# A four-layer image kernel on one core: the diagonal of a scan moved to ACT, pieces of a pipeline at other places, two softplus operations on POOL

## The chip, the cores and the metric

The program runs on one core of a Trainium2 chip. The core has five engines that run side by side, each through its own instructions in order: PE (TensorE: matrix products and, as PEld, the loading of their weights), DVE (VectorE), ACT (ScalarE), POOL (GpSimd) and SP (SyncE, which here issues DMA transfers and does no arithmetic). They wait for each other by semaphores. SBUF is the working memory of 128 partitions, PSUM the memory that PE writes into; POOL works on SBUF alone.

The metric is the device time of one execution in microseconds (us), smaller being better. Of the kernel before there are ten timed runs: the median is 7649.24 us, the lowest 7633.43 and the highest 7655.76.

## The reference, cut to what matters

Four layers follow each other on an input of 4 images with 96 channels and 64 x 64 pixels, all in 32-bit floating point. The change touches layers 0 and 1; layer 2 (two windowed attentions and an MLP) and layer 3 (Fourier magnitudes, a deformable convolution) stay as they are.

Layer 0 runs two state-space blocks over the 4096 pixels of an image taken as a sequence:

```python
h = (seq - mu) * rsqrt(var + EPS) * ln_g + ln_b
xs, z = split(h @ in_w)                       # 192 channels each
xc = silu(causal 4-tap convolution of xs + conv_b)
dt, Bm, Cm = split(xc @ xproj_w)              # 6, 16 and 16 columns
delta = softplus(dt @ dt_w + dt_b)
dA  = exp(delta * A)                          # 192 channels x 16 states
dBx = delta * Bm * xc
hstates[t] = dA[t] * hstates[t-1] + dBx[t]    # a scan along the sequence
y = sum over states of hstates * Cm + Dp * xc
seq = seq + (y * silu(z)) @ out_w
```

After both blocks come a product with fus_w, a batch norm and the residual. Dp is a vector over the channels: "Dp * xc" is a product with a diagonal matrix.

Layer 1 is a depthwise 5 x 5 convolution with silu, and then a smaller state-space form with 4 states:

```python
delta = softplus(dt_w @ dts + dt_b)
log_dA = maximum(delta * A, log(1e-9))
P = exp(cumsum(log_dA))
hs = P * cumsum(delta * Bs * xs / maximum(P, 1e-9))
y = sum over states of hs * Cs + xs * Ds
```

Both softplus functions are computed as relu(v) + log(1 + exp(-|v|)), with a correction: w = 1 + e is rounded, and e - (w - 1), what the rounding lost, is given back. So there is a relu (dl or dx), a term w - 1 - e that is subtracted from it, and a logarithm that is added to it.

## The kernel before, in words

**Layer 0** works in units. A unit is one image, one of the two blocks and one chunk of 512 pixels: 4 x 2 x 8 = 64 units, one after the other. Its 192 x 16 states lie in 24 tiles of 128 partitions x 512: eight steps m = 0 to 7, in each of which three tiles (index q) lie side by side. Even steps serve channels 0 to 95 (hf = 0), odd ones channels 96 to 191, and two steps share one of four groups of states (nq).

One step is, in the order of the data: DVE multiplies the replicated input xR by the broadcast Bb into a tile bt of 128 x 1536 (L577); ACT computes three decays a_ps = exp(A * dR) (L588); DVE runs three scans over bt (L604), each with one decay; ACT copies the last column to the carry (L612); POOL multiplies bt by Cb (L613); PE sums the states into yp (L630, "collect"). bt has four buffers and a_ps three.

The order of the work is written out by hand: the program's order is the order of each engine's queue. Every step has four quarters q = 0 to 3. Quarters 0 to 2 issue a scan each, and then the decay of the scan two places on. Quarter 3 issues the sums of two steps earlier (`collect(v - 2)`), then the carry and L613 of this step (`outputs`), and then L577 of the next (`inputs`).

What a unit needs before its scans is made by the generator `prepare`, whose pieces end at each `yield`. Piece n of a unit's preparation runs at the head of quarter n - 16, counted in quarters from the start of the unit before it: one piece in each quarter, over two units, an empty piece being a pause. The condition is `taken[w] <= 4 * v + q - PERIOD * (w - 1) + AHEAD`, with a PERIOD of 32 quarters and 16 AHEAD. In order, the pieces that the prediction names, with the places (step, quarter) that they have before:

- (4,0) PE product L418; (4,2) ACT L423 and L424; (4,3) PE L427 and a small copy on POOL, L432; (5,1) ACT L435 and L436; (5,2) DVE L438; (5,3) ACT L440; (6,0) to (6,3) the convolution's products, PE L447; from (7,0) ACT L456 and PE L459, by turns.
- In the next unit: (0,0) to (0,2) ACT L463, L466, then L468 with L469; (0,3) ACT L471 and POOL L472, the silu's last product; (1,2) PE L478; (2,0) ACT L482 and a store by SP; (2,1) PE L488; (2,3) two ACT L495 (the absolute values of softplus); (3,0) ACT L497 (exponential) and L498 (relu of the first half); (3,1) L500 (relu of the second half) and two L502 (the 1 + e); (3,2) two DVE L505 (w - 1 - e); (3,3) two ACT L511 (logarithms) and POOL L512; (4,0) POOL L514 and stores by SP; (4,1) POOL L519 and stores by SP; (4,2) ACT L524; (4,3) ACT L526 and the six loads dR and xR of the first half by SP; (5,0) ACT L531 and POOL L532.

Beside these, at fixed places: L641 (yp of the unit before, to SBUF by ACT) at (1,1) and (2,1), POOL L646 at (2,2) and then the products L650 and L652 and what follows them, and the loads of the second half and of Cb from (5,2) on. In three units `pooled` puts a long reduction (L400) on DVE. At the first chunk of every image and block `collect` makes the diagonal `skips[hf]` = ident * Dp with a DVE operation (L624), which PE multiplies by xc (L627).

**Layer 1** works in 16 chunks of 1024 pixels, with three tiles each: 48 steps v, i = v mod 3. In a step `sums` does the first cumulative sum of the next step (DVE L902, a product and a maximum, and the scan L903, whose other input is a broadcast one; POOL L907; ACT L908 to L910; POOL L911), and `states` the second one of this step (DVE L925, the scan L926, ACT L929, DVE L930 and L933, and PE's sums L937 and spreads L319). L950 ends a chunk. Around them lie three places n = 0, 1, 2: place 0 is before `sums`, place 1 between `sums` and `states`, place 2 after `states`.

The preparation of a chunk has nine pieces: 1 transposes (PE L857); 2 silu (ACT L862) with the loading of its table and of the next one; 3 a product (PE L319); 4 absolute value, exponential and 1 + e (ACT L874 to L876); 5 relu (DVE L878); 6 w - 1 - e (DVE L880) and its subtraction (L881); 7 the logarithm (ACT L883); 8 its addition (DVE L885) and six loads of rl by SP; 9 the product dx (POOL L889) and six loads of rx by SP. The set `slots` gives the places, with the step counted from the first step of the chunk before.

Of the kernel before, what the change touches and what calls it, by code (L numbers as in the profile page):

```python
# [12 lines left out]
AF = mybir.ActivationFunctionType  # L13
ALU = mybir.AluOpType
# [4 lines left out]
B, C, H, W = 4, 96, 64, 64  # L19
# [320 lines left out]
def layer0(k, X):  # L340

    tc, nc, ins = k.tc, k.nc, k.ins
# [4 lines left out]
    with ExitStack() as es:  # L347
# [46 lines left out]
        def mm():  # L394
            return pm.tile([128, NB], F32, name="mm_ps", tag="mm")
# [18 lines left out]
        def prepare(b, i, ch, st, before):  # L414
# [6 lines left out]
            e = p2.tile([C, 2, T], F32, name="e")  # L421
# [13 lines left out]
            nc.scalar.activation(p[:C], p[:C], AF.Ln, bias=k.eps5[:C])  # L435
            nc.scalar.activation(p[:C], p[:C], AF.Exp, scale=-0.5)  # L436
            yield
            nc.vector.scalar_tensor_tensor(d, d, k.v(f"ln_g{i}"), p[:C], ALU.mult, ALU.mult)  # L438
            yield
            nc.scalar.activation(h[:, 3:], d, AF.Identity, bias=k.v(f"ln_b{i}"))  # L440
# [2 lines left out]
            ps = []  # L443
# [42 lines left out]
            ps = [mm() for _ in range(2)]  # L486
# [4 lines left out]
            e = p2.tile([C, 2, T], F32, name="e")  # L491
            dx = p1.tile([C, 2, T], F32, name="dx")
            bias = [k.v(f"dt_b{i}{hf}") for hf in range(2)]
            for hf, p in enumerate(ps):
                nc.scalar.activation(e[:, hf], p[:C], AF.Abs, bias=bias[hf])  # L495
            yield
            nc.scalar.activation(e, e, AF.Exp, scale=-1.0)  # L497
            nc.scalar.activation(dx[:, 0], ps[0][:C], AF.Relu, bias=bias[0])  # L498
            yield
            nc.scalar.activation(dx[:, 1], ps[1][:C], AF.Relu, bias=bias[1])  # L500
            for hf, p in enumerate(ps):
                nc.scalar.activation(p[:C], e[:, hf], AF.Identity, bias=k.one[:C])  # L502
            yield
# [5 lines left out]
            w = p1.tile([C, 2, T], F32, name="w")  # L509
# [46 lines left out]
        carries, bts, Bbs, dec, skips = {}, {}, {}, {}, {}  # L556

        def at(v):

            u, m = divmod(v, NT)  # L560
            return (sts[u], units[u], *divmod(m, 2))
# [55 lines left out]
        def collect(v):  # L617

            st, (b, i, ch), nq, hf = at(v)
            if nq == 0:  # L620
                yp = st["yp", hf] = py.tile([C, T], F32, name="yp")
                if ch == 0:
                    skips[hf] = p1.tile([C, C], F32, name=f"skip{hf}")
                    nc.vector.tensor_scalar(  # L624
                        skips[hf], k.ident[:C, :C], k.v(f"Dp{i}{hf}"), None, ALU.mult
                    )
                nc.tensor.matmul(yp, skips[hf], st["xc"][:, hf], start=True, stop=False)  # L627
            bt = bts.pop(v)
            for q in range(NG):
                nc.tensor.matmul(  # L630
                    st["yp", hf][32 * q : 32 * q + 32],
                    red,
                    bt[:, q],
                    start=False,
                    stop=nq == NQ - 1,
                )
# [92 lines left out]
        scale, shift = batch_norm(k, wp, stats, k.v("bn_g"), k.v("bn_b"))  # L729
# [11 lines left out]
def batch_norm(k, pool, stats, gamma, beta):  # L741

    nc = k.nc
    mv = pool.tile([C, 2], F32, name="bn_mv")
    nc.vector.bn_aggr(mv, stats.rearrange("c b n s -> c (b n s)"))
    sc = pool.tile([C, 2], F32, name="bn_sc")
    nc.scalar.activation(sc[:, 0:1], mv[:, 1:2], AF.Sqrt, bias=k.eps5[:C])
    nc.vector.reciprocal(sc[:, 0:1], sc[:, 0:1])
    nc.vector.tensor_mul(sc[:, 0:1], sc[:, 0:1], gamma)
    nc.vector.tensor_mul(sc[:, 1:2], mv[:, 0:1], sc[:, 0:1])  # L750
    nc.vector.tensor_sub(sc[:, 1:2], beta, sc[:, 1:2])
    return sc[:, 0:1], sc[:, 1:2]
# [5 lines left out]
def layer1(k, X):  # L758

    tc, nc, ins = k.tc, k.nc, k.ins  # L760
    T, G, NT = 1024, 8, 3
    NP, NCH = H // 2, L // T
    with ExitStack() as es:
# [10 lines left out]
        with tc.tile_pool(name="l1s", bufs=1) as sp, tc.tile_pool(  # L774
# [4 lines left out]
            ps = pp.tile([C, C], F32, name="wd1_ps")  # L779
# [4 lines left out]
        with tc.tile_pool(name="l1t", bufs=3) as tp, tc.tile_pool(  # L784
# [11 lines left out]
            for i in range(B * NP // 4):  # L796
                b, p0 = divmod(4 * i, NP)
                ps = pp.tile([128, 4, C], F32, name="ft_ps", tag="t")
# [8 lines left out]
            for g in range(C // G):  # L807
                t = bands.pop(0)
                for h in range(2):
                    c0 = G * g + 4 * h  # L810
                    ps = pp.tile([128, 4, B, NP], F32, name="cv_ps", tag="t")
# [29 lines left out]
        def packed(dst, src):  # L841

            for n in range(4):
                r = C * n
                while r < C * n + C:
                    at = r % 128
                    m = min(C * n + C - r, 128 - at)
                    c0 = r - C * n
                    nc.sync.dma_start(dst[r // 128][at : at + m], src[c0 : c0 + m])
                    r += m  # L850

        def prepare(u):

            b, ch = divmod(u, NCH)
            ps = pm.tile([C, T], F32, name="xs_ps", tag="mm")
            for j in range(T // 128):
                nc.tensor.transpose(  # L857
                    ps[:, 128 * j : 128 * j + 128], F[:, :, b, T // 128 * ch + j], k.ident
                )
            yield  # L860
            x = xs[u] = p3.tile([C, T], F32, name="xs")
            nc.scalar.activation(x, ps, AF.Silu, bias=k.v("l1_conv_b"))  # L862
            nc.scalar.preload_act_table_set("natural_log_exp_and_others")
            yield
            ps = pm.tile([128, T], F32, name="dt_ps", tag="mm")
            k.mm(ps, [(Wd, x)])
            ps = ps[:C]
            yield
            bias = k.v("l1_dt_b")
            e = p1.tile([C, T], F32, name="sp_e")  # L870
            w = p1.tile([C, T], F32, name="sp_w")
            dl = p1.tile([C, T], F32, name="dl")
            dx = p1.tile([C, T], F32, name="dx")
            nc.scalar.activation(e, ps, AF.Abs, bias=bias)  # L874
            nc.scalar.activation(e, e, AF.Exp, scale=-1.0)
            nc.scalar.activation(w, e, AF.Identity, bias=k.one[:C])  # L876
            yield
            nc.vector.tensor_scalar(dl, ps, bias, 0.0, ALU.add, ALU.max)  # L878
            yield
            nc.vector.scalar_tensor_tensor(e, w, -1.0, e, ALU.add, ALU.subtract)  # L880
            nc.vector.tensor_sub(dl, dl, e)  # L881
            yield
            nc.scalar.activation(w, w, AF.Ln)  # L883
            yield
            nc.vector.tensor_add(dl, w, dl)  # L885
            rl[u] = [p3.tile([128, T], F32, name="rl", bufs=4) for _ in range(NT)]
            packed(rl[u], dl)
            yield
            nc.gpsimd.tensor_mul(dx, dl, x)  # L889
            rx[u] = [p3.tile([128, T], F32, name="rx", bufs=4) for _ in range(NT)]  # L890
            packed(rx[u], dx)
            yield

        def sums(v):

            u, i = divmod(v, NT)
            if u % NCH == 0 and i == 0:
                carry[u // NCH] = p2.tile([128, 2, NT], F32, name="carry1")
                nc.vector.memset(carry[u // NCH], 0.0)
            c = carry[u // NCH]  # L900
            t = lp[v] = p2.tile([128, T], F32, name="lp")
            nc.vector.tensor_scalar(t, rl[u][i], A[:, i : i + 1], LOG_EPS, ALU.mult, ALU.max)  # L902
            nc.vector.tensor_tensor_scan(  # L903
                t, one.to_broadcast([128, T]), t, c[:, 0, i : i + 1], ALU.mult, ALU.add
            )
            e = q[v] = p3.tile([128, T], F32, name="q1")
            nc.gpsimd.tensor_scalar(e, t, LOG_EPS, None, ALU.max)  # L907
            nc.scalar.copy(c[:, 0, i : i + 1], t[:, T - 1 : T])  # L908
            nc.scalar.activation(e, e, AF.Exp, scale=-1.0)
            nc.scalar.activation(t, t, AF.Exp)  # L910
            nc.gpsimd.tensor_mul(e, e, rx[u][i])  # L911
# [42 lines left out]
        with tc.manual_schedule():  # L954
            ahead = {}

            for _ in prepare(0):
                pass
            sums(0)
            spread(0, 0)  # L960
            spread(0, 1)
            slots = {(-3, 2), (-2, 0), (-2, 1), (-1, 0), (-1, 1), (-1, 2), (0, 0), (0, 1), (0, 2)}

            def slot(v, n):

                for u in range(U):
                    if u and (v - NT * (u - 1), n) in slots:
                        if u not in ahead:
                            ahead[u] = prepare(u)
                        next(ahead[u], None)  # L970

            for v in range(-NT, 0):
                for n in range(3):
                    slot(v, n)
            for v in range(V):
                u, i = divmod(v, NT)
                slot(v, 0)
                if v + 1 < V:
                    sums(v + 1)
                if i == 0 and u:  # L980
                    result(u - 1)
                slot(v, 1)
                states(v)
                slot(v, 2)
            result(U - 1)
# [1229 lines left out]
```

## Time and profile before

The profiled execution took 7655.72 us, with a span of 7653.9 us from the first to the last instruction; the rest is what lies around the span. It stands 6.5 us above the median of the ten runs. The granted TensorE clock was 0.819 on the mean.

| engine | busy us | share of the span | instructions |
|---|---|---|---|
| PE | 5777.3 | 75% | 24090 |
| DVE | 5789.3 | 76% | 8127 |
| ACT | 3899.7 | 51% | 7624 |
| POOL | 4692.6 | 61% | 2915 |

| stretch, us | DVE busy | ACT busy | POOL busy | PE busy |
|---|---|---|---|---|
| layer 0, 140 to 3240 (3100) | 2903.0 | 2194.6 | 2609.6 | 2385.8 |
| layer 1's steps, 3440 to 4056 (616) | 506.5 | 216.9 | 273.9 | 392.8 |

How lines of the profile are read: a group of instructions has its line in the kernel, engine, operation, what it writes and reads with shapes, how many there are, then busy time in us and mean ns of one, and the idle time of the engine just before them with what ended it. A line of the timeline has the start in us from the span's start, the duration in us, engine, line, operation and shapes, and in brackets the idle time before it with its releaser. A line of the waits has who waited for whom, us in total, times, and the longest. Instructions of one engine that follow each other may overlap by some hundredths of a microsecond in the records.

### The profile page before, as it was taken

The page shows a single profiled execution, that of the slowest core. Times are in us where ns is not written, and L with a number is a line of the kernel's source. Part 1 is how long each engine was busy: PE and PEld are TensorE (multiplying, and loading weights), DVE is VectorE, ACT ScalarE, POOL GpSimd, SP SyncE. Part 2 cuts the span into 40 slices and gives each one's busy share as a digit, 9 for nine tenths or more (in the row PEclk, how much of TensorE's full clock was granted, in tenths as well). Part 3 has the DMA queues.
Part 4 walks back from the last instruction along what each step waited for, and adds up shares of the span by engine and source line. Part 5 has one row for each costly group of instructions (what it writes and reads, how often), then busy time and mean ns, then how long its engine had stood idle before and what let it go on. Part 6 is the DMA issues. An engine that isn't in the chain of part 4 may idle for free.

```text
span 7653.9 us, 76610 instructions
## 1 busy us (share of the span) xinstructions
PE 5777.3 (75%) x24090; PEld 2664.2 (35%) x24090; DVE 5789.3 (76%) x8127; ACT 3899.7 (51%) x7624; POOL 4692.6 (61%) x2915
## 2 busy tenths in 40 slices
PE   4777777777777777756668888898977677777774
PEld 1222222222222222242225546464645534444432
DVE  4999999999999999938886636354644478787886
ACT  3767676777767677633334556465644212121211
POOL 3888888888878888814444524243430077777775
PEclk8888888888888888877887888888888778787886
DMA  3333232233333332252331010000100165656555
GB/s 99 105 105 105 100 104 98 93 105 105 105 105 105 102 103 89 100 157 77 83 83 48 8 30 14 23 21 1 43 17 15 45 189 156 195 150 194 158 157 170
DMA packets 424412, 720.29 MB, mean 94 GB/s; under 512 B 188150, under 2 KB 190254, under 8 KB 419763
## 3 DMA queue, kind: packets, MB, share of 16 engines
q1 hardware_dynamic: 348710, 480.74, 20.2%
q0 software_dynamic: 73968, 227.47, 10.2%
q10 hardware_dynamic: 1328, 7.20, 0.3%
q8 instruction: 191, 3.13, 0.2%
q14 instruction: 215, 1.75, 0.1%
HBM read 567.04 MB, written 97.82 MB: 87 GB/s over the span
## 4 chain that ended last, share of the span: by engine, by line
PE 37%; DVE 25%; ACT 16%; POOL 9%; issue 8%; DMA 5%; SPq 1%; DVEq 0%; POOLq 0%; ACTq 0%
DVE bt L604 6%; PE mm_ps L447 6%; POOL sm L2010 6%; DVE bt L577 3%; PE mm_ps L478 3%; PE yp L630 3%; PE sc_ps L1086 3%; ACT a_ps L588 3%; PE pT_ps L1135 2%; DMA sm<-table,ix 2%; PE o_ps L1155 2%; POOL xc L472 2%; DVE prod L2027 1%; DVE sm L2028 1%; PE bc_ps L319 1%
## 5 line engine op out<-in xcount | busy, mean ns | idle before, releaser
L604 DVE TENSOR_TENSOR_SCAN bt<-a_ps,carry,bt 128x512 f32<-128x512 f32 x1536 | 1872.0, 1267 | 67.0 <-ACT a_ps L588 12.3
L613 POOL TENSOR_TENSOR bt<-bt,Cb 128x1536 f32<-128x1536 f32 x512 | 1756.7, 3440 | 200.9 <-ACT carry L612 179.5
L2010 POOL DMA_INDIRECT sm<-table,ix x1152 | 1099.5, 954 | 736.0 <-DVE gs L1771 347.1
L588 ACT ACTIVATE a_ps<-dR,w_l_A_log 128x512 f32<-128x512 f32 x1536 | 1040.0, 685 | 611.7 <-DVE bt L604 603.8
L577 DVE TENSOR_TENSOR bt<-xR,Bb 128x1536 f32<-128x1536 f32 x512 | 884.6, 1728 | 28.0 <-DMA xR<-spread 16.4
L630 PE MATMUL yp<-bt,w_c_red 128*32 128x512 f32 x3072 | 595.2, 671 | 12.7 <-POOL bt L613 12.7
L1123 POOL TENSOR_TENSOR p<-p,rs 128x392 f32<-128x392 f32 x384 | 311.6, 839 | 475.5 <-DVE rs L1121 401.3
L570 PE MATMUL Bb<-dbl,w_c_seln 128*128 128x512 f32 x512 | 353.7, 779 | 323.8 <-DVE bt L577 323.8
L447 PE MATMUL mm_ps<-h,Wk 96*128 96x512 f32 x1024 | 487.5, 632 | 140.6 <-issue 87.4
L2048 PE MATMUL sT_ps<-ident,sd 128*128 128x128 f32 (+1 forms) x896 | 210.5, 352 | 299.7 <-DVE sd L2031 179.5
L319 PE MATMUL bc_ps<-xs,w_l_bc 96*128 96x512 f32 x384 | 241.8, 763 | 214.4 <-DVE q L930 214.4
L1110 ACT ACTIVATE p<-p,rs 128x196 f32<-128x196 f32 x768 | 342.7, 449 | 83.1 <-DVE rs L1100 82.9
L447 PEld LDWEIGHTS mm_ps<-h,Wk 96*128 96x128 f32 x1024 | 200.8, 201 | 433.7 <-issue 433.2
L2027 DVE TENSOR_TENSOR prod<-sm,cws 128x960 f32<-128x960 f32 (+1 forms) x256 | 270.8, 1058 | 56.4 <-DMA sm<-table,ix 50.9
L472 POOL TENSOR_TENSOR xc<-xc,gate 96x1024 f32<-96x1024 f32 x64 | 150.1, 2345 | 263.4 <-ACT carry L612 234.1
L2049 ACT COPY sT<-sT_ps 128x512 f32<-128x512 f32 (+1 forms) x256 | 121.8, 476 | 367.9 <-PE sT_ps L2048 367.9
L1933 PE MATMUL yb_ps<-X,w_l_base_w 96*128 96x504 f32 (+3 forms) x576 | 304.1, 692 | 0.3 <-ACT go L1947 0.3
L1143 DVE COPY pT<-pT_ps 98x512 f32<-98x512 f32 x256 | 175.9, 687 | 150.1 <-PE pT_ps L1135 142.7
L570 PEld LDWEIGHTS Bb<-dbl,w_c_seln 128*128 128x128 f32 x512 | 88.9, 218 | 550.0 <-DVE bt L577 489.5
L907 POOL TENSOR_SCALAR q<-lp 128x1024 f32<-128x1024 f32 x48 | 133.6, 2784 | 236.6 <-DVE lp L903 236.6
L1100 DVE CUSTOM_DVE_ANT_0 p<-sc_ps,bias 128x196 f32<-128x196 f32 x768 | 233.7, 353 | 47.6 <-PE sc_ps L1086 47.1
L2028 DVE TENSOR_TENSOR sm<-sm,cws 128x960 f32<-128x960 f32 (+1 forms) x256 | 267.7, 1046 | 0.0
(374 smaller groups left out, 12695.5 us busy)
## 6 DMA issues: line engine op xcount, KB each, us to landing
dR<-spread SPq DMA_DIRECT2D x384, 256.0 KB
xR<-spread SPq DMA_DIRECT2D x384, 256.0 KB
Cb<-out_states SPq DMA_DIRECT2D x256, 256.0 KB
spread<-w SPq DMA_DIRECT2D x128, 192.0 KB
spread<-dx SPq DMA_DIRECT2D x128, 192.0 KB
table<-xT SPq DMA_DIRECT2D x256, 96.0 KB
own<-vd SPq DMA_DIRECT2D x512, 36.8 KB
toep<-l_toep SPq DMA_DIRECT2D x12, 1536.0 KB
```

The costliest lines, as they stand in the source:

```text
L319: self.nc.tensor.matmul(ps[:, s], lhsT, rhs[:, s], start=k == 0, stop=k == len(terms) - 1)
L447: nc.tensor.matmul(p, Wk[:, i, t, hf], h[:, t : t + T], start=t == 0, stop=t == 3)
L570: nc.tensor.matmul(Bb, seln[:, nq], st["dbl"], start=True, stop=True)
L577: nc.vector.tensor_mul(bt, st["xR", hf, None], Bb.unsqueeze(1).to_broadcast([128, NG, T]))
L588: nc.scalar.activation(dec[n], st["dR", hf, q], AF.Exp, scale=A[:, i, nq, hf, q : q + 1])
L604: nc.vector.tensor_tensor_scan(t, dec.pop(n), t, carry_of(v)[:, q : q + 1], ALU.mult, ALU.add)
L613: nc.gpsimd.tensor_mul(bt, bt, st["Cb", nq].unsqueeze(1).to_broadcast([128, NG, T]))
L630: nc.tensor.matmul(st["yp", hf][32 * q : 32 * q + 32], red, bt[:, q], start=False, stop=nq == NQ - 1,)
L1110: nc.scalar.activation(ps[n][:, h, i], ps[n][:, h, i], AF.Exp, scale=-1.0, bias=rs[n][:, 0, h, i : i + 1], accum_out=rs[n][:, 1, h, i : i ...
L2010: nc.gpsimd.indirect_dma_start(sm[u][:, t].rearrange("p q c -> p (q c)"), None, samples[m // NN % 2], bass.IndirectOffsetOnAxis(ap=ix[m][: ...
L2027: nc.vector.tensor_mul(p, v[:, :, 2:4], w_[:, :, 2:4])
L2028: nc.vector.tensor_mul(v[:, :, 0:2], v[:, :, 0:2], w_[:, :, 0:2])
```

## The change

It has four parts. In layer 0 the diagonal is made by an ACT operation instead of a DVE one. A `yield` is added before L438, so that the pieces from there on come one quarter later. In the softplus of layer 0 the two relus go one piece to the front of their places (the first to the absolute values, the second to the exponential), and a `yield` goes behind the second, in place of the one before it. In layer 1 two operations of softplus go from DVE to POOL, and the set of places of the preparation is another.

```diff
             nc.scalar.activation(p[:C], p[:C], AF.Exp, scale=-0.5)
             yield
+            yield
             nc.vector.scalar_tensor_tensor(d, d, k.v(f"ln_g{i}"), p[:C], ALU.mult, ALU.mult)
...
                 nc.scalar.activation(e[:, hf], p[:C], AF.Abs, bias=bias[hf])
+            nc.scalar.activation(dx[:, 0], ps[0][:C], AF.Relu, bias=bias[0])
             yield
             nc.scalar.activation(e, e, AF.Exp, scale=-1.0)
-            nc.scalar.activation(dx[:, 0], ps[0][:C], AF.Relu, bias=bias[0])
-            yield
             nc.scalar.activation(dx[:, 1], ps[1][:C], AF.Relu, bias=bias[1])
+            yield
             for hf, p in enumerate(ps):
                 nc.scalar.activation(p[:C], e[:, hf], AF.Identity, bias=k.one[:C])
...
-                    nc.vector.tensor_scalar(
-                        skips[hf], k.ident[:C, :C], k.v(f"Dp{i}{hf}"), None, ALU.mult
+                    nc.scalar.activation(
+                        skips[hf], k.ident[:C, :C], AF.Identity, scale=k.v(f"Dp{i}{hf}")
                     )
...
             nc.vector.scalar_tensor_tensor(e, w, -1.0, e, ALU.add, ALU.subtract)
-            nc.vector.tensor_sub(dl, dl, e)
+            nc.gpsimd.tensor_sub(dl, dl, e)
             yield
             nc.scalar.activation(w, w, AF.Ln)
             yield
-            nc.vector.tensor_add(dl, w, dl)
+            nc.gpsimd.tensor_add(dl, w, dl)
...
-            slots = {(-3, 2), (-2, 0), (-2, 1), (-1, 0), (-1, 1), (-1, 2), (0, 0), (0, 1), (0, 2)}
+            slots = {(-3, 1), (-3, 2), (-2, 1), (-2, 2), (-1, 1), (-1, 2), (0, 0), (0, 1), (0, 2)}
```

## The prediction

> **What bounds the kernel now.** I read the page first: its costliest groups belong to layer 0, where the DVE row of the slices stands at 9. Three of the page's groups:
>
> ```profile
> L604 DVE TENSOR_TENSOR_SCAN bt<-a_ps,carry,bt 128x512 f32<-128x512 f32 x1536 | 1872.0, 1267 | 67.0 <-ACT a_ps L588 12.3
> L613 POOL TENSOR_TENSOR bt<-bt,Cb 128x1536 f32<-128x1536 f32 x512 | 1756.7, 3440 | 200.9 <-ACT carry L612 179.5
> ...
> L577 DVE TENSOR_TENSOR bt<-xR,Bb 128x1536 f32<-128x1536 f32 x512 | 884.6, 1728 | 28.0 <-DMA xR<-spread 16.4
> ```
>
> Next the groups kept apart by shape, then whom DVE waited for from 140 to 3240 us:
>
> ```profile
> L624 DVE TENSOR_SCALAR skip<-ident,vec 96x96 f32<-96x96 f32 x16 | 79.1, 4941 | 0.0
> ```
> ```profile
> DVE e L438 <- issue: 62.9, 55, 1.4
> DVE e L505 <- ACT mm_ps L502: 52.9, 53, 1.2
> DVE e L438 <- ACT mm_ps L436: 16.6, 7, 2.6
> ```
>
> Scans and products fill DVE. What is not work is 79.5 us before L438, 52.9 before L505, and most of L624's 79.1. The timeline shows why 96 columns take 5 us:
>
> ```profile
> 522.87 2.35 POOL L646 TENSOR_TENSOR xc<-xc,sz 96x1024 f32<-96x1024 f32 x1
> 522.88 5.79 DVE L624 TENSOR_SCALAR skip<-ident,vec 96x96 f32<-96x96 f32 x1
> ...
> 525.16 3.44 POOL L613 TENSOR_TENSOR bt<-bt,Cb 128x1536 f32<-128x1536 f32 x1
> ```
>
> L624 ends at 528.67, 0.07 us after POOL falls idle: it was held through two POOL operations.
>
> Then one regular unit by engine (POOL, PE, ACT, DVE). Its first scan starts at 665.23; that is my zero.
>
> ```profile
> 670.43 2.34 POOL L472 TENSOR_TENSOR xc<-xc,gate 96x1024 f32<-96x1024 f32 x1 [3.19 <-ACT carry L612]
> 672.74 6.82 POOL L613 TENSOR_TENSOR bt<-bt,Cb 128x1536 f32<-128x1536 f32 x2
> ```
> ```profile
> 672.83 3.78 PE L478 MATMUL mm_ps<-xc,w_l_xp 96*128 96x512 f32 x4 [0.19 <-POOL xc L472]
> 676.54 1.76 PE L630 MATMUL yp<-bt,w_c_red 128*32 128x512 f32 x6
> ```
> ```profile
> 678.36 0.58 ACT L641 COPY xc<-yp 96x512 f32<-96x512 f32 x1 [0.54 <-PE yp L630]
> ...
> 684.07 1.29 ACT L502 ACTIVATE mm_ps<-e,ones 96x512 f32<-96x512 f32 x2
> ```
> ```profile
> 679.54 1.73 DVE L577 TENSOR_TENSOR bt<-xR,Bb 128x1536 f32<-128x1536 f32 x1
> ...
> 684.78 1.30 DVE L505 SCALAR_TENSOR_TENSOR e<-mm_ps,e 96x512 f32<-96x512 f32 x2 [0.95 <-ACT mm_ps L502]
> ```
>
> One chain runs through all of them: L472, L478, L630, L641, ACT's queue, L502, L505. It reaches DVE 0.95 us late.
>
> In layer 1 DVE's wait is for ACT; the second fence is one such wait, then POOL and DVE where they met:
>
> ```profile
> DVE q L930 <- ACT carry L929: 94.6, 48, 6.6
> ```
> ```profile
> 3652.06 1.11 ACT L862 ACTIVATE xs<-xs_ps,vec 96x1024 f32<-96x1024 f32 x1 [8.18 <-PE xs_ps L857]
> ...
> 3656.65 1.22 DVE L930 TENSOR_TENSOR q<-lp,bc_ps 128x1024 f32<-128x1024 f32 x1 [4.93 <-ACT carry L929]
> ```
> ```profile
> 3437.92 3.65 POOL L907 TENSOR_SCALAR q<-lp 128x1024 f32<-128x1024 f32 x1 [13.84 <-DVE lp L903]
> ...
> 3445.05 2.35 POOL L889 TENSOR_TENSOR dx<-dl,xs 96x1024 f32<-96x1024 f32 x1
> ```
> ```profile
> 3446.07 1.87 DVE L902 TENSOR_SCALAR lp<-rl,w_l_A 128x1024 f32<-128x1024 f32 x1
> ```
>
> L902 lasts 0.75 elsewhere; here it waits out L889. L907 lasts 2.76 elsewhere; here L885, a DVE product of two SBUF tiles begun 0.18 us earlier, held it 0.9.
>
> **Layer 0, the diagonal.** Sixteen operations leave DVE, fifteen of them 78.5 us long. A unit with two of them lasts 58.1, others 47.6 (L447 starts at 891.06, 949.37 and 996.97 in the chain). On ACT the nearest rows are L612 (3 columns, 0.19) and L423 (512 columns, 0.56); I take 0.25, in ACT's queue of the walk below, where it delays L505 by as much.
>
> **Layer 0, the added yield.** The second hunk adds and removes one, so L438's piece and all thirty behind it run a quarter later, with their POOL operations and SP's stores and loads.
>
> L438 goes behind a scan of 1.19 us: its 1.13 us stall goes, with that scan as cover. -1.1 a unit.
>
> L472 leaves step 0, quarter 3, for step 1, quarter 0, and on POOL falls behind step 0's L613. Walk from zero with the spacings of the ACT timeline: the decay after the first scan 1.32, L466 1.94, decay 2.88, L468 3.49, L469 3.97, L612 5.02, so L613 5.28 and, 3.39 later, L472 at 8.67 instead of 5.20: 3.47 late. PE runs in order, so L478 and L630 are as late: L630 ends at 16.54, not 13.07. Two things wait for it. L577 of step 3 writes the bt buffer that this L630 frees (there are four): due at 14.31, it starts at 16.6. L641 starts at 16.60, and behind it ACT has two decays, L612, two L495, L498, a decay, L497, L500 and now one more decay (0.62) before L502: 6.32 us in all. The first L502 lasts 0.68, so L505 starts at 23.63, where it was 19.55. In DVE's order it stands one scan (1.19) later, so the unit loses 4.08 - 1.19 = 2.9. What is late next is L512 and its stores.
>
> PE is idle 3.6 us before the later L478, so L488 may run at L478's slow pace (3.78 instead of 1.98), 1.4 us more at L495. Bounds 0 and 1.4; I take 0.3, nearer to the warm row, which also follows L478 directly. Unit: 2.9 - 1.1 + 0.3 = +2.1. The lower bound is +0.5 (L613 at 3.95, right behind the scans), the upper +3.2.
>
> SP: L519 ends at 35.5 instead of 31.5, so the first half's six loads are issued by 40.2 and needed by L577 at 47.6. Six times 256 KB at the 300 GB/s of that burst take 5 us: hidden by steps 5 to 7, with 2 us to spare; beyond that each microsecond is one of DVE.
>
> Sum of layer 0: 64 units, less 8 with the diagonal and 3 with L400 (4.34 us of DVE that cover the new stall), are 53 x 2.1 = +111; 3 x -1.1 = -3; the diagonal units go from 58.1 to 47.6 + 2.1 + 0.3, 7 x -8.1 and about -5 for the first, -62. Together +46.
>
> **Layer 1.** Quarter 2 of a step and quarter 0 of the next have nothing between them, so of the moved places only the first changes the order: the transposes L857 go ahead of the step's products. From L930 to L930 the three steps take 14.10, 14.9 (14.04 to 15.67) and 10.64. With L862 early the middle one could reach 10.64.
>
> L881 and L885 save DVE 1.22 each and cost POOL 2.35 each (L889, same shape). POOL now has, in order, L881 beside L902 and L903, and L911, L885, L889 beside the next L902 and L903. L902 waits for POOL, as its row shows. L903 reads two SBUF tiles, like L885; that a POOL product holds it is not shown. Bounds 0 and 2.35 each time; I take 2.0, by L902's row, which waited to L889's end. First step: 14.10 - 2.44 + 2.0 = 13.7. Middle: 10.64 + 1.1 (L902, to L885's end) + 2.0 = 13.75. So -1.55 a chunk, 14 x = -22, and +3 in the first chunk, where nothing overlaps: -19. The rl and rx loads start some 6 us later, still about 10 us ahead of the L902 that needs them: hidden by the middle step. Without the hold: 12.15 and 11.5, -75 + 3 = -72.
>
> A rule speaks against this part: the Trainium skill, "SBUF — State Buffer", section "Who interferes with whom", says that a VectorE instruction with two SBUF inputs contends with a GpSimd instruction that reads SBUF and that the later one blocks fully. L907's 0.9 us agrees; by the rule the layer's part is the -19, without it the -72.
>
> **The sum.** +46 - 19 = +27. The profiled execution took 7655.7 us (span 7653.9), 6.5 above the median of 7649.2; on the median that makes 7676.
>
> **The rivals.** *The scan is not held.* Layer 1 gives -72 and the sum -26: 7623, faster. For it: L885 beside L907's later part lost nothing. Against: L907's 3.65 row. It decides once L903's two waits average under about 0.9 us. *The late L472 is covered.* If L472's lateness cost nothing, L438 would give -1.1 x 60, L505 (one scan later, one decay more: 1.19 - 0.62) -0.57 x 53, the diagonal -78: -174, with layer 1 -193, 7456. For it: POOL idles 3.19 us before L472. Against: POOL's order. The sum's sign turns where the lateness falls under 3.0 us, since 60 units carry it. *PE stays cold.* L488 slow in every unit: +1.1 x 53 more, 7734. For it: L478 is slow at 3.78 throughout.
>
> **How the numbers follow.** Forecast 0.45, own range 7645 to 7705 (L472's lateness 3 to 4 us, L488 between its paces). Scan not held 0.2, L472 covered 0.15, PE cold 0.2. The range 7600 to 7740 takes in all but the covered case and the ends. About 0.2% (15 us) is what a measurement can tell. Slower: 0.2 cold + 0.3 of the forecast = 0.5. Faster: 0.15 + 0.18 + 0.03 = 0.36. Same 0.14.
>
> **What would show it.** L624 on ACT under 0.6 us; no idle before L438; L472 starting about 8.7 us after the unit's first scan, behind L613; L577 of step 3 waiting about 2 us for L630; L505's wait at or above today's; regular units near 49.7 us; L903 longer than 2.35 where L881 or L889 runs; L930's wait after L862 gone. I am wrong if regular units shorten, which says that the chain from L472 has cover that I did not see, or if L903 stays at 2.35.

## The result and the profile after

The changed kernel takes 7808.44 us (median of 8 runs) beside 7646.59 us for the kernel before (28 runs): a ratio of 1.0212, with a 95% interval of 1.0201 to 1.0224. It is slower by some 162 us. The forecast was 7676 us, with a range of 7600 to 7740.

Lines of the changed kernel have numbers higher by one than those of before from L438 on. The profiled execution after has a span of 7811.1 us, 157.2 longer than before. I cut both spans by the records of DVE: layer 0 is the stretch from the start of the first scan (L604) to the end of the last, layer 1 the stretch from the first L930 to the last.

| stretch, us | before | after | change | predicted |
|---|---|---|---|---|
| layer 0 | 3151.4 | 3322.6 | +171 | +46 |
| layer 1 | 606.8 | 586.8 | -20 | -19 |
| all else | 3895.7 | 3901.7 | +6 | 0 |

The loss is in layer 0 alone. From the costliest groups of the page after:

```profile
L605 DVE TENSOR_TENSOR_SCAN bt<-a_ps,carry,bt 128x512 f32<-128x512 f32 x1536 | 1862.8, 1266 | 71.7 <-ACT a_ps L589 22.1
...
L578 DVE TENSOR_TENSOR bt<-xR,Bb 128x1536 f32<-128x1536 f32 x512 | 889.5, 1737 | 260.9 <-PE yp L631 128.9
L448 PE MATMUL mm_ps<-h,Wk 96*128 96x512 f32 x1024 | 608.9, 751 | 219.5 <-issue 121.1
```

DVE's scans and products take about what they took; the product in front of a step's scans now waits 260.9 us, where it had waited 28.0. Whom DVE waited for from 140 to 3330 us (us in total, times, the longest):

```profile
DVE bt L578 <- PE yp L631: 126.7, 58, 2.5
DVE bt L578 <- issue: 88.8, 43, 3.2
DVE e L506 <- ACT mm_ps L503: 85.2, 61, 1.5
DVE e L439 <- ACT mm_ps L436: 40.9, 62, 0.8
DVE bt L578 <- POOL bt L614: 24.4, 17, 1.4
```

By place in the unit, with the shortest waits that this view leaves out, these are four: L578 of step 3 (128.9 us), L506 (86.6), L439 (40.9) and L578 of the next unit's step 0 (116.2; most of it in the second and the fifth line). The kernel before had 52.9 at L505, 79.5 at L438 and 11.5 at the last place. One unit on DVE, whose first scan starts at 738.30:

```profile
754.69 1.75 DVE L578 TENSOR_TENSOR bt<-xR,Bb 128x1536 f32<-128x1536 f32 x1 [2.00 <-PE yp L631]
...
761.60 1.30 DVE L506 SCALAR_TENSOR_TENSOR e<-mm_ps,e 96x512 f32<-96x512 f32 x2 [1.42 <-ACT mm_ps L503]
...
774.24 0.74 DVE L439 SCALAR_TENSOR_TENSOR e<-e,vec,mm_ps 96x512 f32<-96x512 f32 x1 [0.63 <-ACT mm_ps L436]
...
787.82 1.75 DVE L578 TENSOR_TENSOR bt<-xR,Bb 128x1536 f32<-128x1536 f32 x1 [1.46 <-issue]
```

The same unit on POOL, on ACT and at its end on PE, then POOL at L512 and PE at L447 in the kernel before:

```profile
743.64 3.43 POOL L614 TENSOR_TENSOR bt<-bt,Cb 128x1536 f32<-128x1536 f32 x1 [3.81 <-ACT carry L613]
747.02 2.35 POOL L473 TENSOR_TENSOR xc<-xc,gate 96x1024 f32<-96x1024 f32 x1
...
763.04 3.44 POOL L614 TENSOR_TENSOR bt<-bt,Cb 128x1536 f32<-128x1536 f32 x1 [2.00 <-issue]
766.44 2.36 POOL L513 TENSOR_TENSOR dx<-dx,e 96x1024 f32<-96x1024 f32 x1
```
```profile
768.83 1.06 ACT L525 ACTIVATE gate<-sz 96x1024 f32<-96x1024 f32 x1 [0.65 <-POOL dx L513]
...
773.63 0.57 ACT L436 ACTIVATE mm_ps<-mm_ps 96x512 f32<-96x512 f32 x1
...
776.00 0.72 ACT L441 ACTIVATE h<-e,vec 96x512 f32<-96x512 f32 x1
```
```profile
776.87 7.09 PE L448 MATMUL mm_ps<-h,Wk 96*128 96x512 f32 x12 [3.26 <-ACT h L441]
783.89 1.06 PE L631 MATMUL yp<-bt,w_c_red 128*32 128x512 f32 x6
784.88 1.98 PE L448 MATMUL mm_ps<-h,Wk 96*128 96x512 f32 x4
786.70 1.02 PE L571 MATMUL Bb<-dbl,w_c_seln 128*128 128x512 f32 x2
```
```profile
686.16 2.36 POOL L512 TENSOR_TENSOR dx<-dx,e 96x1024 f32<-96x1024 f32 x1 [0.85 <-DVE e L505]
688.48 3.43 POOL L613 TENSOR_TENSOR bt<-bt,Cb 128x1536 f32<-128x1536 f32 x1
```
```profile
699.89 7.11 PE L447 MATMUL mm_ps<-h,Wk 96*128 96x512 f32 x16 [1.85 <-ACT h L440]
```

L473 starts 8.72 us after the first scan, behind L614, as predicted. But the lateness goes further than I followed it. L513 has moved behind an L614 too: before, it ran ahead of step 3's and began 0.08 us after the end of L505; now it runs behind it and begins 3.54 us after the end of L506 (medians over 63 units). ACT's L525 writes a buffer that L513 must first have read: by the program two buffers are used in turn, and L423, which kept its place and now comes ahead of L525, takes the other one. So L525 waits (54 times, 35.1 us in all), and L436, L439 and L441 are late behind it. PE is then idle for 3.26 us before L448 and takes for twelve records what sixteen took before. L571, the Bb of the next unit, comes last, and DVE's first product of that unit waits for it.

Layer 1 from 3450 to 4150 us, on DVE:

```profile
L904 DVE TENSOR_TENSOR_SCAN lp<-ones,carry,lp 128x1024 f32<-128x1024 f32 x44 | 160.5, 3647 | 1.6
...
L931 DVE TENSOR_TENSOR q<-lp,bc_ps 128x1024 f32<-128x1024 f32 x43 | 52.5, 1221 | 32.3 <-ACT carry L930 32.3
...
L903 DVE TENSOR_SCALAR lp<-rl,w_l_A 128x1024 f32<-128x1024 f32 x45 | 49.5, 1101 | 9.1 <-DMA rl<-dl 9.1
```

The scan grew from 2351 ns (its row before reads as that of the run slots below) to 3647 ns, and L931's wait fell from 94.6 to 32.3. From L931 to L931 a chunk's three steps take 13.75, 13.66 and 10.64 us; 13.7, 13.75 and 10.64 were predicted.

### The profile page after: what moved, and what is told of

Read it like the earlier page. It is cut to its first block, busy times and chain, and to the rows that moved or that the text cites. A ratio compares the mean times of both kernels' runs of the same rounds, so it can differ in the third digit from the quotient of the medians.

```text
span 7811.1 us, 76760 instructions
## 1 busy us (share of the span) xinstructions
PE 5834.0 (75%) x24090; PEld 2700.1 (35%) x24090; DVE 5763.9 (74%) x8079; ACT 3910.1 (50%) x7640; POOL 4779.0 (61%) x2947
## 4 chain that ended last, share of the span: by engine, by line
PE 25%; DVE 19%; POOL 14%; issue 9%; ACT 8%; DMA 4%; SPq 1%; DVEq 0%; POOLq 0%; ACTq 0%
POOL sm L2011 6%; DVE bt L605 3%; PE sc_ps L1087 3%; DMA sm<-table,ix 2%; PE pT_ps L1136 2%; DVE bt L578 2%; DVE lp L904 2%; POOL bt L614 2%; PE mm_ps L479 2%; PE o_ps L1156 2%; PE mm_ps L448 2%; POOL q L908 2%; DVE prod L2028 2%; DVE sm L2029 1%; ACT a_ps L589 1%
## 5 line engine op out<-in xcount | busy, mean ns | idle before, releaser
L614 POOL TENSOR_TENSOR bt<-bt,Cb 128x1536 f32<-128x1536 f32 x512 | 1758.7, 3440 | 526.6 <-ACT carry L613 279.5
L578 DVE TENSOR_TENSOR bt<-xR,Bb 128x1536 f32<-128x1536 f32 x512 | 889.5, 1737 | 260.9 <-PE yp L631 128.9
L448 PE MATMUL mm_ps<-h,Wk 96*128 96x512 f32 x1024 | 608.9, 751 | 219.5 <-issue 121.1
L631 PE MATMUL yp<-bt,w_c_red 128*32 128x512 f32 x3072 | 586.7, 651 | 17.4 <-POOL bt L614 17.4
L571 PE MATMUL Bb<-dbl,w_c_seln 128*128 128x512 f32 x512 | 331.1, 733 | 230.0 <-DVE bt L578 230.0
L448 PEld LDWEIGHTS mm_ps<-h,Wk 96*128 96x128 f32 x1024 | 233.4, 239 | 602.1 <-issue 583.0
L479 PE MATMUL mm_ps<-xc,w_l_xp 96*128 96x512 f32 x256 | 242.0, 1101 | 246.2 <-POOL xc L473 246.2
L1136 PE MATMUL pT_ps<-ident,p 128*98 128x128 f32 x1536 | 251.1, 303 | 8.7 <-DVE pT L1144 5.8
L2049 PEld LDWEIGHTS sT_ps<-ident,sd 128*128 128x128 f32 (+1 forms) x896 | 124.0, 170 | 373.5 <-ACT sT L2050 149.4
```

Of the source, the lines that this page charges most:

```text
L448: nc.tensor.matmul(p, Wk[:, i, t, hf], h[:, t : t + T], start=t == 0, stop=t == 3)
L479: nc.tensor.matmul(p, xp[:, i, hf], xc[:, hf], start=hf == 0, stop=hf == 1)
L578: nc.vector.tensor_mul(bt, st["xR", hf, None], Bb.unsqueeze(1).to_broadcast([128, NG, T]))
L614: nc.gpsimd.tensor_mul(bt, bt, st["Cb", nq].unsqueeze(1).to_broadcast([128, NG, T]))
L631: nc.tensor.matmul(st["yp", hf][32 * q : 32 * q + 32], red, bt[:, q], start=False, stop=nq == NQ - 1,)
L1136: nc.tensor.transpose(pT[:, i, j], ps[n][:, h, i, 98 * j : 98 * j + 98], k.ident)
```

## The experiments

The theory: the added yield costs all of the loss, because L473 falls behind L614 and everything that hangs on it is late, L448's pace at the end included. The rivals: the other edits of layer 0 carry a part of it; or the late L441 and L448 cost the time by themselves, whatever L473 does; or L448's slow pace is beside the point. The runs were made on several chips. On two of them (the runs warm, slots, both, best3 and warm3) the kernel before takes some 8230 us, because of layers 2 and 3 alone: in slots, which leaves layer 0 as it was, that layer takes 3150 us there too. So times are compared as ratios with the kernel before on the same chip, and stretches as they are. A stretch is that of one profiled execution; runs with the same layer differ by up to 7 us in layer 0 (3144.1 to 3151.4) and 3 us in layer 1 (585.7 to 588.7).

| run | ratio (95% interval) | layer 0, us | layer 1, us |
|---|---|---|---|
| changed kernel | 1.0212 (1.0201-1.0224) | 3322.6 | 586.8 |
| no_yield | 0.9903 (0.9881-0.9925) | 3085.5 | 585.9 |
| diag | 0.9921 (0.9904-0.9938) | 3083.3 | 607.0 |
| l1_part | 0.9973 (0.9960-0.9987) | 3144.1 | 586.0 |
| chain_back | 0.9847 (0.9824-0.9869) | 3049.1 | 586.0 |
| bb_first | 1.0148 (1.0124-1.0172) | 3273.1 | 585.9 |
| warm | 1.0260 (1.0229-1.0291) | 3365.1 | 588.7 |
| warm2 | 1.0191 (1.0173-1.0208) | 3304.8 | 586.9 |
| warm3 | 1.0076 (1.0055-1.0098) | 3216.8 | 585.7 |
| slots | 0.9945 (0.9924-0.9966) | 3150.4 | 548.5 |
| both | 0.9841 (0.9810-0.9872) | 3018.5 | 586.6 |
| best3 | 0.9846 (0.9816-0.9877) | 3069.4 | 550.7 |
| best4 | 0.9745 (0.9726-0.9765) | 3017.9 | 549.4 |
| best5 | 0.9712 (0.9695-0.9729) | 2991.2 | 551.1 |

**The parts one by one.** First the changed kernel without the yield (the diff), then the kernel before with the diagonal alone (the change's hunk at L624) and with layer 1's part alone (its last three changed places).

```diff
             nc.scalar.activation(p[:C], p[:C], AF.Exp, scale=-0.5)
             yield
-            yield
```

> The whole change without the added yield before L439. Theory: the yield alone makes layer 0 longer (wait for L631 at step 3, the longer wait at L506, the late first product of the next unit: some 245 us, against 39 saved at L439), and the diagonal saves about 78 and layer 1 some 20, so 7550 us (7530 to 7575), 1.3% below the kernel before. Rival: the moved relus or the diagonal in ACT's queue carry a part of it; then the time stays above 7600.

> The kernel before with the diagonal on ACT alone. Theory of the prediction's term: 15 units of 58.1 and the like lose a diagonal each, some 7 x 10.3 us and 5 in the first: the layer-0 stretch falls from 3151 to 3075, 7574 us (7560 to 7585). The rival from the run without the yield (66 us saved there, with 22 us more at L505): the diagonal in ACT's queue makes L502 late, and the stretch falls to 3085 only; if instead the moved relus caused the 22 us, the stretch falls to 3064 here.

> The kernel before with layer 1's part alone. Theory: the 20 us by which the stretch from the first L930 to the last became shorter are the whole of it, 7629 us (7620 to 7640). Rival: the layer's part also reaches what follows (7 us were lost behind the last L930 in the profile of the changed kernel); then 7636 or more.

Measured: 7578.1, 7592.1 and 7633.6 us. DVE's wait at L505 from 140 to 3180 us, with the diagonal alone and without the yield:

```profile
DVE e L505 <- ACT mm_ps L502: 73.0, 59, 1.7
```
```profile
DVE e L505 <- ACT mm_ps L502: 73.3, 59, 1.8
```

Layer 0 without the yield is 237 us shorter than with it, so the yield is the loss. The time missed the expected 7550 slightly, and the diagonal says why: alone it saves 68 us, not 76, and L505's wait rises from 52.9 to 75.1 us, short waits included, since the seven units that it shortens wait there too (60 units in place of 53) and the others somewhat longer. Without the yield the stretch is 3085.5 and L505's wait 75.4, so the moved relus cost nothing that can be told. Layer 1's part is worth its 20 us.

**L473 and all behind it back in place, the yield kept.** One yield less behind L464 brings L467 and all behind it back to their old places; L439 to L464 stay a quarter late.

```diff
             nc.scalar.copy(sz[:, 0], zs[0][:C])
-            yield
             gate = p2.tile([C, 2, T], F32, name="gate", tag="e")
```

> The changed kernel, yield before L439 kept, with the yield behind the copy of sz's first half (L464) taken out, so that L467 to L532 return to the places that they had before, while L439 to L464 stay late. Theory: the wait of L578 for L631 (128.9 us) and the growth of L506's wait (about 34) go, the late first product of the next unit stays: 7660 us (7640 to 7690). Rival: the late L441 and L448 carry the loss by themselves, and L578's waits only change their name: above 7730.

Measured: 7540.2 us, far below the 7660 expected. All waits of DVE from 140 to 3150 us above 1 us (in this run L472 and what follows have the line numbers of before):

```profile
DVE e L505 <- ACT mm_ps L502: 57.2, 59, 1.7
DVE bt L577 <- issue: 37.6, 27, 1.4
DVE bt L604 <- ACT a_ps L588: 22.3, 8, 3.9
```

Not only the wait for L630 is gone: the wait at L439 is gone too, and two thirds of the late first product. Layer 0 is 273 us shorter than in the changed kernel and 36 shorter than without any yield. So the yield did what it could do at L439, and the later places of the pieces from L467 on turned it into the loss. The edit puts L473 ahead of step 0's L613 again and L513 ahead of step 3's, and L525 no longer waits. L473 explains the 128.9 us at L631; how much of the rest is due to its lateness, and how much to L513's own place, no run separates. I had expected the late first product to stay; two thirds of it came from these pieces as well, by way of L513, L525 and L441. PE's idle time before L448 fits: on the median of the units it is 1.28 us without the yield, 2.53 us in this run and 3.51 us in the changed kernel.

**Which part of L448 makes Bb late?** Put in front of the last L448, Bb no longer waits for them.

```diff
-                    if q == 1 and v + 1 < V:
+                    if q == 0 and v + 1 < V:
                         states_in(v + 1)
```

> The changed kernel with the broadcast of B for the next step (L571) issued at quarter 0 of a step in place of quarter 1, so that it stands ahead of the last L448 on PE. Theory: the wait of the next unit's first L578 (116 us at step 8, quarter 0) falls to under 20: 7710 us (7690 to 7735). Rival: that product is late by another wait too (POOL's L614 or the bt buffer), and the wait only gets another releaser: above 7770.

Measured: 7764.4 us, between the theory and the rival. DVE's waits at L578 from 140 to 3330 us:

```profile
DVE bt L578 <- PE yp L631: 158.8, 59, 3.1
...
DVE bt L578 <- POOL bt L614: 33.0, 32, 1.3
...
DVE bt L578 <- issue: 7.2, 7, 1.1
```

The wait at the next unit's first product fell from 116.2 to 40.2 us, of which 33.0 are now for POOL's L614, as the rival had it; and that of step 3 for L631 grew from 128.9 to 158.8: where the unit starts earlier, POOL and PE's sums are still where they were, so a part of the wait only moves.

Then the pace. Of the kernel with L473 back, twelve L448 in two units that follow each other, both behind 2.77 us of idle time, and the granted clock (the last but two of the columns) while they ran:

```profile
339.39 7.08 PE L448 MATMUL mm_ps<-h,Wk 96*128 96x512 f32 x12 [2.77 <-issue]
```
```profile
386.95 5.39 PE L448 MATMUL mm_ps<-h,Wk 96*128 96x512 f32 x12 [2.77 <-issue]
```
```profile
339.40:346.40 7.00, 7.00 (x12) 2.75 (x12) 6.79 (x6) 3.33 (x6) 7.00 (x4) 0.76 0.95 321
386.95:392.30 5.35, 5.35 (x15) 2.19 (x16) 5.25 (x5) 2.99 (x6) 5.35 (x3) 1.00 0.92 294
```

In the first the next L577 waits 1.37 us, in the second not at all. In that run 28 units have the slow pace, and 27 L577 of step 0 wait, each behind a slow one. To bring the pace back in the changed kernel I gave PE work that changes nothing, three times.

The first run has three products into free rows of L427's bank; the others have products with zero weights that are added to yp, six in the second (shown) and three in the third.

```diff
             yield
+            for _ in range(3):
+                nc.tensor.matmul(p[C:], center[:, :32], xs, start=True, stop=True)
             nc.scalar.activation(h[:, 3:], d, AF.Identity, bias=k.v(f"ln_b{i}"))
```
```diff
-        fbs = {}
+        fbs, last = {}, [None]
...
-            bt = bts.pop(v)
+            bt = last[0] = bts.pop(v)
...
                         collect(v - 2)
+                        if m == 5 and u + 1 < len(units):
+                            for _ in range(6):
+                                nc.tensor.matmul(
+                                    sts[u]["yp", 1][:32], k.ident[:C, C:], last[0][:C, 2], start=False, stop=False
+                                )
```

> The changed kernel with three idle products more on PE (center's first 32 columns times the pixels, into the 32 free rows of the bank that L427 used, read by nobody), issued in the piece of L441, so that they fill PE's 3.3 us before L448. Theory of the clock: PE is slow in L448 because it idled; then the first twelve L448 take 5.3 us in place of 7.1, the first L578 of the next unit is no longer late (116 us), of which, as with the broadcast of B put in front, about 30 come back at L578 of step 3: 7730 us (7710 to 7760). Rival: L448 is late only because L441 is, at whatever pace: no change, 7795 to 7825.

> The changed kernel with six more products on PE right behind the L631 of step 3 (collected in quarter 3 of step 5): the identity's zero block times that bt, added to yp, so nothing changes in the sum. They wait for nothing but what L631 waited for, and leave PE some 1.2 us idle before L448 in place of 3.3. Theory of the clock: the first twelve L448 take 5.3 us in place of 7.1, the next unit's first L578 waits under 0.3 us in place of 1.5 to 3 (116 us in all), some 30 come back at L578 of step 3, and the layer-0 stretch falls from 3322 to 3255 us or less. Rival: L448 is late because L441 is, at whatever pace; the stretch stays at 3310 or more.

> As the run with six products behind that L631, now with three: there each took 0.89 us and the six reached beyond the arrival of L441's result, so that L448 started late though at the faster pace (twelve in 5.42 us). Three take 2.7 us and leave PE some 0.6 us idle. Theory of the clock: the twelve L448 take 5.3 us and start when h is there, L571 is 1.7 us earlier, the regular unit's wait of 1.46 us for it goes, the 116 us fall to under 25, some 30 come back at L578 of step 3: the layer-0 stretch is 3245 to 3265 us. Rival: only L441's place counts; the wait stays above 80 us and the stretch above 3300.

The first try was slower (ratio 1.0260). Its products waited for L439, the last reader of the tile, so they delayed L448; in 40 units the pace was fast and the wait of the next unit 0.5 to 1.3 us, in 22 the added products were slow themselves and the wait was about 4.6 us or more. The second (1.0191) settled little: six products took 5.3 us, not the 2.1 that I had taken from L631, whose six records in 1.06 us run side by side, and reached beyond h's arrival. The third is the clean one:

```profile
753.53 2.74 PE L720 MATMUL yp<-bt,ident 96*32 96x512 f32 x6
756.99 5.39 PE L448 MATMUL mm_ps<-h,Wk 96*128 96x512 f32 x12 [0.72 <-ACT h L441]
762.31 1.06 PE L631 MATMUL yp<-bt,w_c_red 128*32 128x512 f32 x6
763.30 1.99 PE L448 MATMUL mm_ps<-h,Wk 96*128 96x512 f32 x4
765.12 1.02 PE L571 MATMUL Bb<-dbl,w_c_seln 128*128 128x512 f32 x2
```
```profile
DVE bt L578 <- PE yp L631: 139.3, 59, 2.8
...
DVE bt L578 <- POOL bt L614: 2.9, 2, 1.4
```

The second view has DVE's waits at L578 from 140 to 3320 us. L441 is as late as in the changed kernel (38.1 us after the unit's first scan on the median, 37.6 there), yet the 116.2 us of wait are 2.9, and layer 0 falls by 106 us to 3216.8 (10 us came back at step 3, fewer than I expected). So the late first product is the pace: the late L441 costs next to nothing there once PE is kept at work. 173 us of useless products on PE make the changed kernel 1.3% faster (1.0212 to 1.0076).

**Layer 1's part, taken apart.** The new places alone, on the kernel before:

```diff
-            slots = {(-3, 2), (-2, 0), (-2, 1), (-1, 0), (-1, 1), (-1, 2), (0, 0), (0, 1), (0, 2)}
+            slots = {(-3, 1), (-3, 2), (-2, 1), (-2, 2), (-1, 1), (-1, 2), (0, 0), (0, 1), (0, 2)}
```

> The kernel before with layer 1's new places alone, the two operations of softplus left on DVE. Theory (the scan L903 is held by POOL's products, and the wait at L930 goes by the places): the first step of a chunk stays at 14.10 us, the middle one falls from 14.87 to 10.64 to 11.7, so 14 times 3.2 to 4.2: 7649 less 45 to 59 is 7590 to 7604, better than the whole of layer 1's part. Rival (moving the two operations is what pays): less than 25 us, above 7624.

Measured: layer 1 takes 548.5 us, 58 less than before, and the steps 14.10, 10.64 and 10.64 us for most chunks. The scan and L930's wait from 3270 to 4060 us, first with the places alone, then with the two operations on POOL as well (l1_part):

```profile
L903 DVE TENSOR_TENSOR_SCAN lp<-ones,carry,lp 128x1024 f32<-128x1024 f32 x48 | 112.8, 2351 | 1.7
...
L930 DVE TENSOR_TENSOR q<-lp,bc_ps 128x1024 f32<-128x1024 f32 x48 | 58.6, 1221 | 36.9 <-ACT carry L929 36.9
```
```profile
L903 DVE TENSOR_TENSOR_SCAN lp<-ones,carry,lp 128x1024 f32<-128x1024 f32 x48 | 171.9, 3581 | 1.7
...
L930 DVE TENSOR_TENSOR q<-lp,bc_ps 128x1024 f32<-128x1024 f32 x48 | 58.6, 1221 | 37.7 <-ACT carry L929 37.7
```

Moving two operations of 19.5 and 19.4 us off DVE costs 59.1 us at the scan and 14.6 at L902 (37.0 to 51.6). By the places alone the layer would have gained 58 us; the move to POOL gave 37 of them back.

**Kernels that beat both.** The first has the edits of chain_back and bb_first together. best4 has layer 1's two operations on DVE again beside that (the second diff), and best5 also the pieces from L464 to L472, the silu's last, one quarter earlier (the first). best3 is best4 with L505 a quarter later, behind L511 (the third).

```diff
                 zs.append(z)
-                yield
+                if hf == 0:
+                    yield
...
             nc.gpsimd.tensor_mul(xc, xc, gate)
             yield
             yield
             yield
+            yield
```
```diff
-            nc.gpsimd.tensor_sub(dl, dl, e)
+            nc.vector.tensor_sub(dl, dl, e)
...
-            nc.gpsimd.tensor_add(dl, w, dl)
+            nc.vector.tensor_add(dl, w, dl)
```
```diff
             yield
+            w = p1.tile([C, 2, T], F32, name="w")
+            for hf, p in enumerate(ps):
+                nc.scalar.activation(w[:, hf], p[:C], AF.Ln)
+            yield
             for hf, p in enumerate(ps):
                 nc.vector.scalar_tensor_tensor(
                     e[:, hf], p[:C], -1.0, e[:, hf], ALU.add, ALU.subtract
                 )
-            yield
-            w = p1.tile([C, 2, T], F32, name="w")
-            for hf, p in enumerate(ps):
-                nc.scalar.activation(w[:, hf], p[:C], AF.Ln)
             nc.gpsimd.tensor_sub(dx, dx, e)
```

> The changed kernel with both edits, the yield behind L464 taken out and the broadcast of B at quarter 0. Theory: with L472 back in front of L613 nothing hides behind the late broadcast any more, so the 37.6 us that the first L577 of a unit waited in the run with L472 back all go: 7503 us (7495 to 7515). Rival: as in the run with the broadcast alone, a third of the gain turns up at another wait (L505 or the product of step 3): 7515 to 7530.

> The kernel with both edits, the two operations of layer 1's softplus back on DVE, and in layer 0 the two L505 one quarter later, behind L511 and with L512, so that a scan and a decay lie in between. Theory: the 57 us of wait at L505 go, and layer 1 gives some 30 more: 7415 us (7400 to 7440), 45.8 us for a regular unit, which is DVE's work alone. Rival: L512 on POOL comes later with L505, and with it the stores and the loads of the next unit, so that L577 at step 8 waits for its xR: above 7460.

> The changed kernel with the yield behind L464 taken out, the broadcast of B at quarter 0, and layer 1's two operations back on DVE at the new places. Both gains stand in different stretches, so they add: layer 0 3018 us and layer 1 549 us, in all 191 us under the kernel before, on its time of 7649 that is 7458 (7445 to 7475). Rival: the two are not additive, since the loads of layer 1's first chunk start in layer 0's end: 7480 or more.

> As the kernel with the three edits, and the silu's last three steps (L467 to L472) one quarter earlier still (no yield behind the second L460, one yield more behind L472, so that all behind keeps its place). Theory: POOL, which waits for L471 in that kernel (L472 starts 5.2 or 6.2 us after the unit's first scan), takes L472 at about 4.0; L478, L630 and L641 follow earlier, and L505's 75 us of wait fall to under 30: 7415 us (7400 to 7430). Rival: three ACT operations in one quarter make a decay late, and the scans L604 of the unit's first steps wait for L588 by as much: 7450 or more.

The two edits of the first give 3018.5 us: the 37.6 us that the first product still waited are gone, but the stretch falls by 31 only, since L505's wait grew from 59 to 75. best4 adds layer 1's gain in full, 7462.8 us. best5 reaches 7434.0 us, 0.9712 of the kernel before (0.9695 to 0.9729). Its waits of DVE from 140 to 3095 us above 5 us:

```profile
DVE e L507 <- ACT mm_ps L504: 44.8, 32, 1.7
DVE bt L606 <- ACT a_ps L590: 5.8, 9, 0.7
```

L507 (L505 before) still waits in half of the units, where I had expected under 30 us: in these, L472 starts 5.7 us after the unit's first scan in place of 4.1, since ACT, which works there without a pause, comes to L471 late. best3 lost 51 us against best4 in layer 0: L505 waits nearly as much behind L511 (65.4 us, 75.6 in best4), and the scans wait 70.0 us for decays that the earlier L511 holds up on ACT.

## Why the prediction was wrong, point by point

The direction was right, and layer 1's term to within 1 us. What failed is the added yield of layer 0: by the prediction's steps it costs 53 x 2.1 - 3 + 7 x 2.4 = +125 us, it cost 237.

- **The diagonal: nearly right.** L625 on ACT takes 359 to 381 ns (0.25 taken, under 0.6 as bound). With 2.4 a unit for the yield taken off, -62 is -79; alone it gave -68. L505's wait grew by 22 us, 10 of them in the units it shortened.
- **L472 behind L613: right.** 8.67 predicted, 8.72 measured (8.73 on the median). **L577 of step 3: right**, 2.3 predicted, 2.18 on the mean of 59 units.
- **L505: right in its sum.** Its wait stands at 1.42 where the walk's numbers make 1.5 (0.95 + 0.6).
- **"its 1.13 us stall goes, with that scan as cover": wrong.** 0.63 us of it stay: 40.9 us at L439 in all, where the run without the yield has 82.7. The cover holds only if L436 is on time, and L525 before it on ACT waits for POOL's L513. With L472 and what follows back in place the stall does go altogether.
- **"What is late next is L512 and its stores": the step that failed.** I took L512 as late by L505 alone, some 4 us, followed its stores and stopped. The stores came as predicted (L520 ends at 35.4 us in the unit shown, 35.5 predicted), but L512 is 7.3 us late on the median, since the same quarter puts it behind step 3's L613, as it puts L472 behind step 0's. It also releases the buffer that L524 now gets, which leads to L436, L438, L440, PE's idle time before L447, and the Bb of the next unit. The sum has no term for that last product, and it is 116 us, 1.9 a unit.
- **The added yield, term by term.** Against the run without the yield, DVE's waits change by -42 us at L438, +129 at step 3, +11 at L505 and +116 at the next unit's start: 214 of the 237, by unit -0.7, +2.1, +0.2 and +1.9, where the prediction had -1.1, +2.3, +0.6 and nothing, and +0.3 for L488. Of the other 23 us, 4 are waits at the scans and 5.5 longer products L577; some 13 are not traced. A unit lasts 51.6 us on the median; 49.7 were predicted for a regular one.
- **"PE stays cold"** was a rival for L488, with 7734 us. The slow pace came, but at L448, where the idle time before it grew from 1.85 to 3.26 us in the units shown; L488's pace changed little (631 to 675 ns).
- **"The late L472 is covered"** was priced at 7456. The run with L472 back comes nearest to that case: 7540, since L505 keeps its wait (59 us) and close to half of the units still have the slow L448 (37.6 us at the next unit's first product).
- **"The scan is not held": falsified.** The holds sum to 59 us, two in each of 15 chunks, so 1.97 us each; 2.0 was taken. The rule of the Trainium skill ("SBUF — State Buffer", "Who interferes with whom") that spoke against this part agrees with the 3581 against 2351 ns. The price of this rival does not follow from the terms given: 14.10 - 2.44 is 11.66 and 10.64 + 1.1 is 11.74, where it has 12.15 and 11.5 without a reason; by the terms it is -75 us and not -72.

## What to carry to other kernels

Where the program's order is the order of every queue, moving one piece moves all behind it: before adding a pause, look at each queue for the long operation that the moved piece falls behind, and follow its lateness through released buffers as far as the next unit's first operation, not only to the next stall. If a pause is wanted at one place only, give it back at the next place that has room: the same yield was worth +237 us without that and -36 us with it. An engine that is far from its limit can still set the time by its pace after idling, as PE did here.

## What the runs showed of the hardware

Around 2.5 us of idle time, PE's pace afterwards can be either. Over five kernels (before, changed, no_yield, chain_back, bb_first), each without its first unit, counting a unit's L448 as slow when its first eight records take over 700 ns on the mean: below 2.4 us of idle time 12 of 125 were slow, from 2.4 to 3.0 us 43 of 75, from 3.0 us on 112 of 115. The granted clock over the slow twelve shown above was 0.76, over the fast ones 1.00. The Trainium skill ("TensorE: Matmul & The Clock Gate", Part 1) says that activity is judged in a free-running window of about 3.4 us. A window that runs freely fits the two units above, which have the same 2.77 us and different paces; but 2.77 us is less than the window, so by the records PE need not idle for the whole of it, and no run here shows the window itself. The same page's advice to allow no gaps above some 3 us ("Why this matters for your kernels") would be too generous here: of the gaps from 2.4 to 3.0 us, more than half were followed by the slow pace.

What I had not expected is that products whose result is zero, 2.7 us a unit in PE's idle time, pay 106 us. That a DVE scan whose first input is one broadcast column of SBUF is held by a POOL product was open; it is, for 1.97 us of the product's 2.35.
